# Layer norms by a power on GpSimd instead of Sqrt on ScalarE, and half of a projection's products on ScalarE, in a graph network of four residual layers

## The chip, the cores and the metric

The kernel runs on one core of one Trainium2 chip. The metric is the device time of one execution in microseconds, given as the median of several runs. Four compute engines share the core's on-chip memory (SBUF): TensorE (PE in the profile, with its weight loads as PEld), VectorE (DVE), ScalarE (ACT) and GpSimd (POOL). A fifth sequencer, SyncE (SP), only issues DMAs here. Each engine works through its own queue of instructions in order, and waits there on semaphores of the others. PSUM is the memory into which TensorE writes.

## What is computed

A graph of N = 3327 nodes with 512 features each passes through four layers. Every layer adds the result of a graph operation to its input and normalises each row over its 512 features. Cut to what matters:

```python
def _layernorm(x, axis=-1, eps=1e-5):
    m = jnp.mean(x, axis=axis, keepdims=True)
    v = jnp.var(x, axis=axis, keepdims=True)
    return (x - m) / jnp.sqrt(v + eps)

x = _layernorm(x + gat(x, adj, heads=8))               # layer 0
x = _layernorm(x + sage(x, adj, 64))                   # layer 1
x = _layernorm(x + elu(gat(x, adj, heads=8)))          # layer 2
x = _layernorm(x + elu(gat(x, adj, heads=4)))          # layer 3
```

(The two names stand for the longer functions of the reference.) In `gat`, each head projects x by its own weights to h, forms a score `leaky_relu(si + sj)` for every pair of nodes, masks it by the adjacency, takes the softmax over a row, and multiplies it by h. In `sage`, the mean over the first 64 neighbours of a row is projected, goes through a leaky ReLU and is added to a projection of the row itself. A norm is needed for each of 3327 rows in each of four layers, and with it one factor 1/sqrt(v + eps) a row.

## The kernel before

Rows are padded to 3328, which is NT = 26 tiles of 128 rows; a half is HALF = 13 tiles. The work runs in stages that follow each other; the times are from the start of the profiled span, read off the trace:

- projection of layer 0, to about 124 us;
- attention of layer 0, to about 953;
- layer 1, first part (norm of layer 0, two projections, L1173 to L1245), to about 1161;
- layer 1, second part: for each of 26 slabs of 128 rows, TensorE accumulates mask times features (L1295), `output` (L1270) finishes the slab and calls `norm_rows`, and the projection of layer 2 runs in between as jobs; to about 1600. A mask product kt (L1167, VectorE) is what TensorE takes as weights there;
- attention of layer 2, to about 2395;
- `third` (L1331): finish and norm of layer 2, projection of layer 3; to about 2541. This is called the third projection below, and it has the two kinds of steps that the change touches;
- attention of layer 3, its first half of rows to 2865, its second to 3211. While the second half runs, the first half's rows are finished and normalised as jobs (`later`, L1402), and after it the last rows (L1484 to L1531).

*The norm.* `norm_rows` (L146 to L161) takes one or two tiles. For each: VectorE's bn_stats (L152) and bn_aggr (L153) leave mean and variance in `mv`. Then, once for all of them: ScalarE takes Sqrt of the variance plus eps into `rs` (L154), VectorE takes the reciprocal (L155), and a scalar_tensor_tensor (L158) makes minus mean times factor. Last, ScalarE applies scale and bias to each tile in place (L161). It is called 59 times: 13 times with two tiles in layer 1's first part, 26 times with one tile in its second part, 13 times with two in the third projection, 7 times in the last attention. For the last half of the rows, L1488 and L1526 do the same as L154 with `mv4` and `rs4` (three times), and `factors` (L1468 to L1472) the same as L155 and L158.

*The finish of a layer.* `finish_steps` (L165) loads a tile of attention sums h (from `hd`, on SP) and of the layer's input xr (L177, issued by POOL), multiplies h by the reciprocal row sums (L182, VectorE), takes Exp on ScalarE (L189) for the elu, makes the residual sum in two steps on VectorE (L197, L198) and calls `norm_rows`.

*The third projection* goes over the 26 tiles in pairs. A pair's rows are stored to `x3` (SP). `project1` turns a tile round on TensorE (four transposes to `pt`, L267), ScalarE copies it to SBUF (L268), VectorE sums it for a mean (L269). `project2` multiplies it by the weights into two PSUM banks `pw`, sixteen matmuls (L277): each bank holds two heads of 128 columns and some score columns. ScalarE takes Exp of score columns into `dc` (L278) and copies others (L281). VectorE multiplies each bank by `dc`, a factor for each row and head, into `vt` in SBUF (L283), one instruction for each bank; SP stores `vt` as the value rows (L289). The layers of four and of eight heads share these functions; layer 0 and layer 2 have eight heads of 64 columns.

The pools allow two tiles of each `pw` bank and of `pt`, three of `vt` and `xT`, ten of h, six of xr. ScalarE keeps one set of function tables at a time: where the next function isn't in it, the compiler puts an ACT_TABLE_LOAD ahead.

*The order of the work.* TensorE's order is written by hand: it is in manual schedule, and runs in the order in which the program emits it. On the other engines a scheduler places the instructions by what is ready, apart from those in `tc.keep_in_program_order`, so an edit can move instructions that it doesn't name. The order on an engine is fixed once the kernel is built.

*POOL's order* in layer 1's second part holds loads of carries (`cy`, L1123) and of `xi` (L1272); at the start of the third projection, two memsets (`piece_columns`, L254 and L256); in all stages, xr loads.

Of the kernel before, what the change touches and what calls it, by code (L numbers as in the profile page):

```python
# [7 lines left out]
F32 = mybir.dt.float32  # L8
# [4 lines left out]
AF = mybir.ActivationFunctionType  # L13
ALU = mybir.AluOpType
# [4 lines left out]
P = 128  # L19
LN_EPS = 1e-5  # L20
# [6 lines left out]
def _row_pieces(n):  # L27

    return [(0, n)] if n % 16 == 0 else [(0, n // 16 * 16), (n // 16 * 16, n)]
# [3 lines left out]
def kernel(  # L33
# [10 lines left out]
    nc = tc.nc  # L44
# [21 lines left out]
    const = ctx.enter_context(tc.tile_pool(name="const", bufs=1))  # L66
# [15 lines left out]
    for g in range(4):  # L82
# [6 lines left out]
    nc.gpsimd.memset(onecol[:, 31:32], 1.0)  # L89
    below0 = const.tile([P, 1], F32, name="below0")  # L90
    nc.gpsimd.memset(below0, -200.0)
    eps = const.tile([P, 1], F32, name="eps")
    nc.gpsimd.memset(eps, LN_EPS)
    valid = const.tile([P, 1], F32, name="valid")
    nc.gpsimd.memset(valid, 1.0)
    nc.gpsimd.affine_select(out=valid, in_=valid, compare_op=ALU.is_gt, fill=0.0, base=LAST,
                            pattern=[[0, 1]], channel_multiplier=-1)

    c1 = const.tile([P, 2, 16], F32, name="c1")
    c1a = const.tile([P, 2, 4], F32, name="c1a")  # L100
    iv = ident.rearrange("p (x c) -> p x c", c=8)
# [17 lines left out]
    def load_tile(dst, src, t, eng):  # L119

        if src.shape[0] == N and t == NT - 1 and LAST < P:
            nc.gpsimd.memset(dst, 0.0)
            for a, z in _row_pieces(LAST):
                eng.dma_start(out=dst[a:z, :], in_=src[t * P + a:t * P + z, :])
        else:
            eng.dma_start(out=dst, in_=src[t * P:(t + 1) * P, :])
# [16 lines left out]
            eng.dma_start(out=t[:, :, e, :FW], in_=src[:, e * FW:(e + 1) * FW].rearrange("(c p) m -> p c m", p=P))  # L143


    def norm_rows(pool, ys, t0):  # L146
        n = len(ys)
        st = pool.tile([P, 4, 6], F32, name="st")
        mv = pool.tile([P, 4, 2], F32, name="mv")
        rs = pool.tile([P, 4, 2], F32, name="rs")  # L150
        for s, y in enumerate(ys):
            nc.vector.bn_stats(out=st[:, s, :], in_=y)  # L152
            nc.vector.bn_aggr(out=mv[:, s, :], in_=st[:, s, :])  # L153
        nc.scalar.activation(rs[:, :n, 0], mv[:, :n, 1], AF.Sqrt, bias=eps)  # L154
        nc.vector.reciprocal(rs[:, :n, 0], rs[:, :n, 0])  # L155
        if t0 + n == NT:
            nc.vector.tensor_tensor(rs[:, n - 1, 0:1], rs[:, n - 1, 0:1], valid, op=ALU.mult)
        nc.vector.scalar_tensor_tensor(rs[:, :n, 1], mv[:, :n, 0], -1.0, rs[:, :n, 0],  # L158
                                       op0=ALU.mult, op1=ALU.mult)
        for s, y in enumerate(ys):  # L160
            nc.scalar.activation(y, y, AF.Identity, bias=rs[:, s, 1:2], scale=rs[:, s, 0:1])  # L161
# [3 lines left out]
    def finish_steps(pool, xin, layer, t0, n, hbufs=6, eng=nc.sync, xbufs=None, xpool=None, ebufs=None, pinned=False,  # L165
                     together=False):
        H, D = layer.H, layer.D
        ys, xs, steps = [], [], []

        def load():  # L170
            for t in range(t0, t0 + n):
                xr = xpool.tile([P, F], F32, name="xr", tag="hb") if xpool else \
                    pool.tile([P, F], F32, name="xr", bufs=xbufs)
                h = pool.tile([P, F], F32, name="h", bufs=hbufs)
                load_tile(h, hd, t, eng)
                ys.append(h)
                load_tile(xr, xin, t, nc.gpsimd)  # L177
                xs.append(xr)

        def divide(s):  # L180
            h = ys[s]
            ins = nc.vector.tensor_tensor(h.rearrange("p (h d) -> p h d", h=H), h.rearrange("p (h d) -> p h d", h=H),  # L182
                                          rec[:, t0 + s, :H].rearrange("p (h e) -> p h e", e=1).to_broadcast([P, H, D]),
                                          op=ALU.mult)
            if pinned and t0 > 2:
                tc.keep_in_program_order(ins)
            if layer.elu:
                e = pool.tile([P, F], F32, name="e", bufs=ebufs)
                ins = nc.scalar.activation(e, h, AF.Exp)  # L189
                if pinned and layer.li == 2 and (t0, s) == (2, 0):  # L190
                    tc.keep_in_program_order(ins)
                xs.append(e)

        def add(s):
            h, xr = ys[s], xs[s]
            if layer.elu:
                nc.vector.scalar_tensor_tensor(xr, xs[n + s], 1.0, xr, op0=ALU.min, op1=ALU.add)  # L197
                nc.vector.scalar_tensor_tensor(h, h, 0.0, xr, op0=ALU.max, op1=ALU.add)  # L198
            else:
                nc.vector.tensor_tensor(h, h, xr, op=ALU.add)  # L200

        steps.append(load)
        if pinned or together:
            steps += [lambda s=s: divide(s) for s in range(n)] + [lambda s=s: add(s) for s in range(n)]
        else:
            for s in range(n):
                steps += [lambda s=s: divide(s), lambda s=s: add(s)]
        steps.append(lambda: norm_rows(pool, ys, t0))
        return ys, steps

# [21 lines left out]
    class Layer:  # L232
# [39 lines left out]
        def project2(self, pool, bank, wsb, xT, t):  # L272
            H, D = self.H, self.D
            pw = [bank(e) for e in range(2)]
            for c in range(FC):
                for e in range(2):
                    nc.tensor.matmul(pw[e][:, :FW + H], xT[:, c, :], wsb[:, c, e, :], start=c == 0, stop=c == FC - 1)  # L277
            nc.scalar.activation(self.dc[:, t, :], pw[1][:, FW:FW + H], AF.Exp, scale=ALPHA)  # L278
            vt = pool.tile([P, H, D], F32, name="vt")
            for e in range(2):  # L280
                nc.scalar.copy((self.rc, self.qc)[e][:, t, :], pw[e][:, FW:FW + H])  # L281
                hs = slice(e * H // 2, (e + 1) * H // 2)
                nc.vector.tensor_tensor(vt[:, hs, :], pw[e][:, :FW].rearrange("p (h d) -> p h d", d=D),  # L283
                                        self.dc[:, t, hs].rearrange("p (h e) -> p h e", e=1)
                                        .to_broadcast([P, H // 2, D]), op=ALU.mult)
            vv = vt.rearrange("p h d -> p (h d)")
            n = P if t < NT - 1 else LAST
            for a, z in _row_pieces(n):
                (nc.gpsimd if self.li == 0 else nc.sync).dma_start(out=self.vd[t * P + a:t * P + z, :], in_=vv[a:z, :])  # L289
# [1041 lines left out]
    def third(first):  # L1331
        with tc.tile_pool(name="col3", bufs=1) as cp:
# [5 lines left out]
            with tc.tile_pool(name="p_w", bufs=1, reuse_waits="tile") as wp, \  # L1338
# [23 lines left out]
                for t0 in range(0, NT, 2):  # L1362
# [4 lines left out]
                    for s, y in enumerate(ys):  # L1367
                        t = t0 + s
# [22 lines left out]
            with tc.tile_pool(name="f3", bufs=2) as fp, tc.tile_pool(name="f4", bufs=1) as gp:  # L1391
                g = gp.tile([P, HALF, F], F32, name="g")
                st = gp.tile([P, HALF, 2, 6], F32, name="st4")
                mv = gp.tile([P, HALF, 2], F32, name="mv4")
                rs = gp.tile([P, HALF, 2], F32, name="rs4")
# [71 lines left out]
                def scale(q0, n, keep, every):  # L1467
                    def factors():  # L1468
                        qs = slice(q0, q0 + n)
                        keep(nc.vector.reciprocal(rs[:, qs, 0], rs[:, qs, 0]))  # L1470
                        keep(nc.vector.scalar_tensor_tensor(rs[:, qs, 1], mv[:, qs, 0], -1.0, rs[:, qs, 0],
                                                            op0=ALU.mult, op1=ALU.mult))  # L1472

                    def one(q):
                        y = g[:, q, :]
                        if q % every == 1:
                            keep(nc.scalar.activation(y, y, AF.Identity, bias=rs[:, q, 1:2], scale=rs[:, q, 0:1]))
                        else:
                            keep(nc.vector.tensor_scalar(y, y, rs[:, q, 0:1], rs[:, q, 1:2], op0=ALU.mult, op1=ALU.add))
                        store(y, HALF + q, q)  # L1480

                    return [factors] + [lambda q=q: one(q) for q in range(q0, q0 + n)]

                def slots(q0, n, pt, e):  # L1484
                    keep = tc.keep_in_program_order if e == 1 else lambda ins: ins
                    qs = slice(q0, q0 + n)
                    if e == 2:
                        return [lambda: nc.scalar.activation(rs[:, qs, 0], mv[:, qs, 1], AF.Sqrt, bias=eps)] + \  # L1488
                            scale(q0, n, keep, 3)
                    y = g[:, qs, (NS - 1) * P:]  # L1490
                    h = fp.tile([P, 4, P], F32, name="h", bufs=2)
# [28 lines left out]
                keep = tc.keep_in_program_order  # L1520
                for _, _, parts in lasts:
                    parts[1]()
                for k, (q0, n, parts) in enumerate(lasts):
                    for f in parts[2:]:
                        f()
                    keep(nc.scalar.activation(rs[:, q0:q0 + n, 0], mv[:, q0:q0 + n, 1], AF.Sqrt, bias=eps))  # L1526
                    if k > 0:
                        for f in scale(*lasts[k - 1][:2], keep, 2):
                            f()
# [191 lines left out]
```

## Time and profile before

| | us |
|---|---|
| median of 3 runs (lowest, highest) | 3238.24 (3236.37, 3240.77) |
| the profiled execution | 3230.94 |
| its span in the trace | 3229.1 |
| PE busy | 3137.4 (97%) |
| DVE busy | 2626.5 (81%) |
| ACT busy | 2295.1 (71%) |
| POOL busy | 266.6 (8%) |
| ACT table loads, 145 at 1.283 | 186 |
| of them in the third projection, 32 | 41 |
| Sqrt of `norm_rows` (L154), 59 at 0.295 | 17.4 |
| reciprocals of `norm_rows` (L155), 59 at 0.160 | 9.5 |
| products to `vt` (L283), all three projections, 156 at 0.417 | 58.7 |

The busy time of an engine is the sum of its instructions; register, branch, semaphore and DMA-issuing work isn't in it. A group of instructions in the profile is given as line, engine, operation, the tiles it writes and reads with their sizes, the count, then busy time and mean ns of one, and after a bar the idle time of the engine just before them with what ended most of it. A line of a window gives the busy time of PE, PEld, DVE, ACT and POOL in a stretch of the span (instructions in brackets), then the granted share of TensorE's full clock, the DMA engines' busy share, and GB/s. A line of the waits gives who waited for whom: us in total, times, longest. A line of the chain gives the start, the duration, and the engine and line of a piece of the work that ended last.

### The profile page before, as it was taken

The numbers are of one execution on the slowest core, as the hardware profiler recorded it, in microseconds if no ns is written. First come the engines' busy times: TensorE is split into PE (matmuls) and PEld (weight loads), VectorE is DVE, ScalarE is ACT, GpSimd is POOL, SyncE is SP. The second block draws the span as 40 slices with busy tenths as digits, with TensorE's granted clock in tenths as the row PEclk, the third lists the DMA queues.
The fourth block names the chain that finished last, engine by engine and source line by source line (L and its number), as shares of the span: only waits on it lengthen the run. The fifth ranks groups of instructions, "written<-read, shape, count | busy, mean of one in ns | idle before, by whom it ended". The sixth has DMA issues, their size and how long they took to land. (4 is left out here: it accounts for less than half of the span.)

```text
span 3229.1 us, 44980 instructions
## 1 busy us (share of the span) xinstructions
PE 3137.4 (97%) x17910; PEld 1602.3 (50%) x17910; DVE 2626.5 (81%) x2316; ACT 2295.1 (71%) x1855; POOL 266.6 (8%) x414
## 2 busy tenths in 40 slices
PE   8899999999999999999999999999989999999997
PEld 7643343333334467777744333333347655555444
DVE  5799999999987655555499999999999666677887
ACT  1388888899883234444398988899988655568896
POOL 3110000000000111111220000000011000010110
PEclk9999999999999999999999999999999999999998
DMA  9742113111024345555441111011137211122212
GB/s 360 272 149 80 41 51 137 59 45 42 25 87 138 104 127 133 134 142 152 120 135 42 41 35 39 20 42 42 32 107 242 85 43 43 43 59 89 85 47 69
DMA packets 358321, 301.80 MB, mean 93 GB/s; under 512 B 232756, under 2 KB 291966, under 8 KB 356575
## 3 DMA queue, kind: packets, MB, share of 16 engines
q1 hardware_dynamic: 325727, 187.73, 19.9%
q0 software_dynamic: 26864, 103.50, 10.0%
q10 hardware_dynamic: 5520, 7.69, 0.7%
q8 instruction: 142, 2.33, 0.3%
q14 instruction: 68, 0.56, 0.1%
HBM read 221.97 MB, written 76.84 MB: 93 GB/s over the span
## 5 line engine op out<-in xcount | busy, mean ns | idle before, releaser
L834 ACT ACTIVATE y<-t,bi,sc 128x3328 fp8e4<-128x3328 f32 (+1 forms) x520 | 1336.9, 2604 | 100.0 <-PE pd L811 47.8
L855 PE MATMUL po<-t,vj 128*64 128x448 f32 (+1 forms) x6656 | 1272.9, 522 | 14.6 <-DVE t L833 14.5
L855 PEld LDWEIGHTS po<-t,vj 128*64 128x64 f32 x6656 | 461.0, 137 | 687.8 <-issue 617.6
L470 PE MATMUL po<-t,vj 128*128 128x448 f32 (+1 forms) x1456 | 523.3, 516 | 6.2 <-DVE ob L500 3.6
L408 DVE SCALAR_TENSOR_TENSOR t<-rba,qc,mk 128x1664 f32<-128x1664 f32 (+2 forms) x234 | 408.2, 1753 | 127.7 <-PE po L470 88.2
L413 ACT ACTIVATE y<-t,bi,sc 128x1664 fp8e4<-128x1664 f32 (+2 forms) x234 | 374.3, 1617 | 182.5 <-DVE t L408 170.8
L470 PEld LDWEIGHTS po<-t,vj 128*128 128x128 f32 x1456 | 272.1, 190 | 241.5 <-issue 149.8
L833 DVE SCALAR_TENSOR_TENSOR t<-rba,qc,mask 128x3328 f32<-128x3328 f32 (+1 forms) x130 | 381.1, 2987 | 5.7 <-PE po L855 4.9
L833 DVE SCALAR_TENSOR_TENSOR t<-rbb,qc,mask 128x3328 f32<-128x3328 f32 (+1 forms) x130 | 379.9, 2982 | 6.8 <-PE po L855 3.2
L833 DVE SCALAR_TENSOR_TENSOR t<-rbb,qc,mk 128x3328 f32<-128x3328 f32 (+1 forms) x130 | 379.2, 2981 | 6.7 <-PE po L855 4.5
L833 DVE SCALAR_TENSOR_TENSOR t<-rba,qc,mk 128x3328 f32<-128x3328 f32 (+1 forms) x130 | 379.7, 2986 | 5.7 <-PE po L855 3.4
L1295 PE MATMUL acc<-zs,kt 128*128 128x512 f32 x1352 | 360.2, 420 | 0.0
L277 PE MATMUL pw<-wsb,xT 128*128 128x264 f32 (+1 forms) x1248 | 301.7, 397 | 8.8 <-DVE vt L283 7.3
L1295 PEld LDWEIGHTS acc<-zs,kt 128*128 128x128 f32 x1352 | 256.0, 190 | 51.8 <-PE pk L1146 0.8
L811 PE MATMUL pd<-y,sden 128*32 128x384 fp8e4 (+1 forms) x3328 | 270.2, 343 | 0.0
L277 PEld LDWEIGHTS pw<-wsb,xT 128*128 128x128 f32 x1248 | 242.1, 197 | 50.9 <-issue 6.5
L1153 ACT CAST pk<-cy 128x512 f32<-128x512 bf16 x169 | 99.1, 587 | 222.6 <-DVE kt L1167 216.1
L1167 DVE SCALAR_TENSOR_TENSOR kt<-pk,mb 128x512 fp32r<-128x512 f32 x169 | 115.5, 684 | 115.4 <-PE pk L1164 114.2
L811 PEld LDWEIGHTS <-sden 128*32 128x32 bf16 x3328 | 89.1, 95 | 165.3 <-issue 149.9
L283 DVE TENSOR_TENSOR vt<-pw,dc 128x256 f32<-128x256 f32 x156 | 58.7, 417 | 70.5 <-ACT dc L278 64.7
L1193 PE MATMUL pz<-wn,xT 128*128 128x512 f32 x208 | 96.0, 605 | 5.9 <-DMA wn<-in_wnT_dram 5.5
L1123 POOL DMA_DIRECT2D cy<-ctd x91 | 68.0, 747 | 371.1 <-ACT pk L1153 304.7
(249 smaller groups left out, 2234.2 us busy)
## 6 DMA issues: line engine op xcount, KB each, us to landing
raw<-in_adjT_dram SPq DMA_DIRECT2D x67, 416.0 KB
vj<-v SPq DMA_DIRECT2D x169, 128.0 KB
cy<-ctd POOLq DMA_DIRECT2D x78, 256.0 KB, 4.3
h<-hd SPq DMA_DIRECT2D x61, 256.0 KB
v<-vt SPq DMA_DIRECT2D x50, 256.0 KB
xr<-x POOLq DMA_DIRECT2D x45, 256.0 KB, 3.2
md<-mask SPq DMA_DIRECT2D x26, 416.0 KB
mb<-md SPq DMA_DIRECT2D x169, 64.0 KB
```

What stands on the lines that cost most here:

```text
L277: nc.tensor.matmul(pw[e][:, :FW + H], xT[:, c, :], wsb[:, c, e, :], start=c == 0, stop=c == FC - 1)
L408: ins = nc.vector.scalar_tensor_tensor(t[:, :w], rb[:, lo:lo + w], self.qc[:, j, h:h + 1], mask_at[0](j, i0 + lo, w), op0=ALU.max, op1=ALU ...
L413: nc.scalar.activation(y[:, :w], t[:, :w], AF.Sigmoid, bias=self.bi[:, j, h:h + 1], scale=self.sc[:, j, h:h + 1], saturate=False)
L470: nc.tensor.matmul(po[c][k * D:(k + 1) * D, :z - a_], vj[:, j % 2, k * D:(k + 1) * D], ts[k][:, a_:z], start=j == 0, stop=j == NT - 1)
L811: nc.tensor.matmul(pd[c][32 * kk:32 * kk + 32, :w_], lhsT, rhs, start=(kk, c) not in seen, stop=last and j == NT - 1)
L833: nc.vector.scalar_tensor_tensor(to, ro, self.qc[:, j, h:h + 1], m, op0=ALU.max, op1=ALU.mult)
L834: nc.scalar.activation(yo, to, AF.Sigmoid, bias=self.bi[:, j, h:h + 1], scale=self.sc[:, j, h:h + 1], saturate=False)
L855: nc.tensor.matmul(po[c][k * D:(k + 1) * D, :z - a_], vj[:, j % 2, x_:x_ + D], t[:, k, a_:z], start=j == 0, stop=j == NT - 1)
L1153: nc.scalar.copy(pks[k % 2], carry[b, t // 4 * 4][:, t % 4:t % 4 + 2, :])
L1167: nc.vector.scalar_tensor_tensor(kt, pk, NEIGHBOURS, mb[:, t:t + 2, :], op0=ALU.is_le, op1=ALU.mult)
L1193: nc.tensor.matmul(pz, xT[:, c, :], wn[:, c, :], start=c == 0, stop=c == FC - 1)
L1295: nc.tensor.matmul(acc, kts[b, t][:, s * P:(s + 1) * P], zs(t, c), start=t == 0 and c == 0, stop=t == NT - 1 and c == 1)
```

## The change

Three edits go together.

1. The factor 1/sqrt(v + eps). A new function `rsqrt` has POOL add eps to the variance and raise the sum to the power of -0.5 (tensor_scalar, then tensor_tensor with a constant tile that is filled with -0.5). `norm_rows`, L1488 and L1526 call it in place of ScalarE's Sqrt; VectorE's reciprocals (L155 and L1470) are dropped, and the constant tile `eps`. The two calls for the last half were or could be held in program order; the new ones are not.
2. In `project2` of layer 3 only, bank 1 (heads 2 and 3) is taken out of PSUM by ScalarE, with one multiplication by a column of `dc` for each head, in place of one VectorE instruction for the bank. Bank 0 stays on VectorE.
3. The xr loads of layer 2's finish (26 tiles) are issued by SP in place of POOL.

```diff
+    power = const.tile([P, 8], F32, name="power")
+    nc.gpsimd.memset(power, -0.5)
...
+    def rsqrt(out, var):
+        n = out.shape[-1]
+        return [nc.gpsimd.tensor_scalar(out, var, LN_EPS, None, op0=ALU.add),
+                nc.gpsimd.tensor_tensor(out, out, power[:, :n], op=ALU.pow)]
+
     def norm_rows(pool, ys, t0):
...
-        nc.scalar.activation(rs[:, :n, 0], mv[:, :n, 1], AF.Sqrt, bias=eps)
-        nc.vector.reciprocal(rs[:, :n, 0], rs[:, :n, 0])
+        rsqrt(rs[:, :n, 0], mv[:, :n, 1])
...
-                load_tile(xr, xin, t, nc.gpsimd)
+                load_tile(xr, xin, t, nc.sync if layer.li == 2 else nc.gpsimd)
...
                 hs = slice(e * H // 2, (e + 1) * H // 2)
+                if self.li == 3 and e:
+                    for h in range(hs.start, hs.stop):
+                        nc.scalar.mul(vt[:, h, :], pw[e][:, (h - hs.start) * D:(h - hs.start + 1) * D], self.dc[:, t, h:h + 1])
+                    continue
                 nc.vector.tensor_tensor(vt[:, hs, :], pw[e][:, :FW].rearrange("p (h d) -> p h d", d=D),
...
-                        keep(nc.vector.reciprocal(rs[:, qs, 0], rs[:, qs, 0]))
...
-                        return [lambda: nc.scalar.activation(rs[:, qs, 0], mv[:, qs, 1], AF.Sqrt, bias=eps)] + \
+                        return [lambda: rsqrt(rs[:, qs, 0], mv[:, qs, 1])] + \
...
-                    keep(nc.scalar.activation(rs[:, q0:q0 + n, 0], mv[:, q0:q0 + n, 1], AF.Sqrt, bias=eps))
+                    rsqrt(rs[:, q0:q0 + n, 0], mv[:, q0:q0 + n, 1])
```

All lines are those of the kernel before.

More of the change, by code (lines that the diff above doesn't have):

```diff
@@ L91 @@
     nc.gpsimd.memset(below0, -200.0)
-    eps = const.tile([P, 1], F32, name="eps")
-    nc.gpsimd.memset(eps, LN_EPS)
     valid = const.tile([P, 1], F32, name="valid")
```

## The prediction

> **What bounds the kernel now.** I read the page's totals first, then the sliced utilisation, then the windows, the waits and the chain of the stage that the change touches most.
>
> ```profile
> PE 3137.4 (97%) x17910; PEld 1602.3 (50%) x17910; DVE 2626.5 (81%) x2316; ACT 2295.1 (71%) x1855; POOL 266.6 (8%) x414
> ```
>
> TensorE (PE) is busy for 97% of the span: 91.7 of 3229.1 us are idle, and no edit here removes a matmul. Only idle PE can be won. Time off ACT or DVE is worth nothing where PE is full, as in the layer-1 stage, where 26 of the 59 norms are (first line: PE 320 of 320 us). It can count in the third projection, 2395 to 2542 us (the others; columns are PE, PEld, DVE, ACT, POOL, clock, DMA share, GB/s):
>
> ```profile
> 1180.00:1500.00 320.00, 320.00 (x1394) 240.38 (x1393) 173.94 (x338) 141.68 (x252) 59.68 (x86) 1.00 0.55 140
> 2395.00:2431.00 36.00, 23.29 (x114) 16.85 (x111) 29.93 (x64) 25.50 (x47) 10.81 (x18) 0.81 0.80 252
> 2431.00:2458.00 27.00, 27.00 (x139) 23.47 (x138) 25.20 (x65) 22.01 (x50) 3.22 (x6) 1.00 0.88 291
> 2458.00:2485.00 27.00, 20.45 (x98) 15.79 (x97) 24.44 (x65) 22.23 (x47) 3.78 (x7) 0.89 0.64 206
> 2395.00:2542.00 147.00, 126.31 (x615) 102.42 (x612) 118.36 (x279) 114.14 (x231) 21.06 (x39) 0.93 0.62 204
> ```
>
> PE is idle for 12.7 us at the start and 6.6 us in the middle, and the clock falls after each (0.81, 0.89). DVE and ACT are near full there. What PE waits for, and who holds DVE:
>
> ```profile
> PE pt L267 <- ACT h L161: 11.8, 4, 8.3
> DVE vt L283 <- ACT dc L278: 11.7, 5, 3.7
> ```
>
> The chain of waits shows ACT's table loads between the norms (2463 to 2468):
>
> ```profile
> 2458.92 0.69 DVE xsum L269
> 2461.57 1.52 ACT h L161 x2
> 2463.11 1.28 ACT L278
> 2465.14 1.28 ACT L154
> 2466.74 1.28 ACT L278
> 2468.11 0.81 ACT h L161
> ```
>
> The groups of table loads and of the norm's Sqrt, over the kernel:
>
> ```profile
> L154 ACT ACT_TABLE_LOAD x45 | 57.7, 1283 | 41.3 <-DVE mv L153 40.8
> L278 ACT ACT_TABLE_LOAD x33 | 42.3, 1283 | 0.6
> L154 ACT ACTIVATE rs<-mv,eps 128x2 f32<-128x2 f32 (+1 forms) x59 | 17.4, 295 | 17.3 <-DVE mv L153 16.6
> ```
>
> **What the Trainium skill says.** "ScalarE: Activation LUTs", section What ACT_TABLE_LOAD costs, gives about 1283 ns per load plus a drain of about 1380. The trace agrees on the load; it shows no such drain (the Sqrt that follows the load of 2402.06 starts at 2403.35), so I count 1.28 us per switch. The same section prices an ACTIVATE at 186 ns + 0.833 ns a column, 93 more per pointer operand, with 93 overlapped back to back. L301 (256 columns from PSUM, constant scale) shows 386 ns against 399 by that rule, so it fits. "GPSIMD Engine Reference", section 3.1, gives 2.6 cycles an element for two-input operations and two software dispatch hops; 8 elements would be nothing, so dispatch sets the price. No page prices power there. Section 8 says that GpSimd shares its SBUF interfaces with VectorE; the trace agrees in kind: L384, one form of TENSOR_SCALAR on POOL, takes 682 to 2683 ns.
>
> **The change, part by part.**
>
> *Removed.* Every Sqrt goes (59 in the groups, 3 in the last half), so that ACT no longer alternates Sqrt with Exp. The built instruction order has 59 table loads against 145: 86 x 1.28 = 110 us of ACT, 32 of the old ones (41 us) in the third projection; 13 Sqrts (3.8) go there too. DVE loses 62 reciprocals of 0.16 us (13, so 2.0 us, in the third projection) and, at layer 3, one of two L283 per tile: 26 x 0.416 = 10.8 us.
>
> *Added on ACT.* 52 products of 128x128 with a pointer scale. By the skill's rule an estimate of 186 + 107 + 93 = 386 ns, 293 if overlapped; I take 0.33: 17 us. ACT in the third projection: 114 - 36 (about 28 loads) - 4 + 17 = 91 of 147 us.
>
> *Added on POOL.* 62 pairs, add eps then power. The trace shows no such operation. Per norm let P be the time from the variance to the factor, both hand-offs in. Below: memset 0.095 and affine_select 0.185 on 128x1, twice, with hand-offs, give 0.6. Above: two L384 at their longest, 5.4 us. I take 1.2 (two at about 0.4 and three hand-offs), and keep 0.6 and 5 for the range. It replaces 1.28 + 0.30 + 0.16 = 1.74 where a load was due, 0.46 where not.
>
> *DVE's new wait.* The next instruction but one on DVE (L158) waits for POOL in order; one of about 0.6 us lies between. Behind it queue the next residual additions and, in layer 1, the mask products kt for which PE waits.
>
> *Third projection, the sum.* PE at full rate takes 3.51 (pw) + 0.44 (pt) = 3.95 us a tile, 102.7 for 26. DVE now takes, at starts 0.60 apart (two L198 in 1.20): 5 x 0.60 + 2 x 0.38 + 0.15 + 0.16 = 4.07, so it is the slower engine. Without the second L283 and the halved reciprocal it is 3.6, with P - 0.6 = 0.6 us of stall per pair 3.9: just at PE's 3.95. Thus:
> - Start: the first norm's variance is there at 2402.8, but its reciprocal waits in DVE's order to 2405.55 and L158 to 2408.97, behind an L182 that waits 2.65 us for its load. In the new order L158 directly follows, so PE starts near 2405, not 2410. The second norm's POOL pair is queued behind the memsets of sden and sm (2.0 + 0.8 us from 2416.2), ready near 2417, not 2423. PE runs without gaps from about 2424 instead of 2430: -6.
> - Middle: PE's 6.6 us of idle came from three loads in a row (3.8 us) and DVE's lag. I count 5 of it: -5.
> - End: the last dc (L278) sat behind two loads (2531.67, 2534.76): -2 to -3.
> - Clock and rounding: -1.
>
> Together -14 (-6 if the stalls only shift, -19 if PE is full to the end). The xr loads move from POOL to SP (26 x 0.54 us of issue): SP has the stores and loads of the stage in its order, two xr loads sit between value loads at the end of layer 2's attention. Those value loads wait for PE to free their buffers until 2352 anyway, and SP's own work in the stage is issue only; I take 0, at worst +2. The value store now waits for ACT too: it is needed only after the stage.
>
> *Layer 3's attention.* PE is full to 2865 and waits 10.4 us after; seven norms of the first half lose up to two loads each there, ACT being 65 to 78 of 83 us busy. PE's gaps at 2949, 3033, 3040 and 3147 us are only partly behind these. I take -2 (+3 to -5).
>
> *Layer 1.* 13 norms at its start, 26 inside: PE is full after 1000 us. POOL's power stands before the weight load wn at 954, for which PE waits 5.5 us: +0.7. DVE already waits 18.2 us (21 times) for the Sqrt there with PE full: 0. If that cover were gone, it would cost 26 x (P - 0.46) = 19 us at 1.2. On POOL the pair stands behind the xi load and the cy loads; the xi load of the slab near 1311 us was issued at 1311.00, its variance came at 1312.41, so nothing holds the pair.
>
> *Tail.* Last factors: load and Sqrt out, two POOL operations in: 0 (0.5 either way).
>
> **Sum.** -14 - 2 + 0.7 = -15.3. The profiled run took 3230.94 us (span 3229.1 and 1.84 around it), so 3215.6; it stands 7.3 us below the median of the runs, 3238.24. From the median: **3223 us**.
>
> **The rivals.**
>
> *R1, slower: power on POOL is long.* From P = 4.5 us the third projection gains nothing: a pair takes DVE 7.2 + 3.9 = 11.1 us, 144 for 13, against 146 used now. At P = 5 it is 151: +5. In layer 1 the kt wait of DVE after the factor is about 2.5 us and one kt (0.68), so each slab loses 5 - 3.2 = 1.8 us, 47 for 26; PE's buffers hold perhaps half: +24. Sum +29: 3267 us. For it: L384's 2.7 us, power's price unknown. Against: two elements a partition only, and POOL is 8% busy.
>
> *R2, same: the stage is bound by its transfers or by the order.* DMA share is 0.88 at 291 GB/s in the one gapless stretch, and four L182 wait 5.3 us for h. Then only the start (-3) and the tail (-2) remain: 3233 at P near 1, 3238 if DVE's stall eats them; I put it at 3235. For it: SP now issues xr too. Against: PE ran at full rate at that share.
>
> *R3, more: all gaps close.* The third projection at 102.7 us from 2405, -19, layer 3 -5: about 3213 us. Against: several h loads are late whatever ACT does.
>
> *R4, no effect off the path:* ACT is 71% busy and PE 97%, so 110 us of ACT are hidden. True for layers 1 and 0, but the waits above end in ACT, so I fold its chance into R2.
>
> **How the numbers follow.** Forecast 3216 to 3231 (P from 0.6 to 1.8, third projection -9 to -19): 0.55. R3, 3206 to 3216: 0.12. R2 with R4, 3231 to 3241: 0.19. R1, above 3241: 0.14. About 0.2% (6.5 us) can be told from no change, so faster means under 3231.8. Faster: 0.55 + 0.12 + 0.02 of R2's edge = 0.69; same 0.17; slower 0.14. The range leaves out a third of R3 below and most of R1 above: 3210 to 3243.
>
> **What would show it.** Right: table loads in the third projection from 32 to under 8; the window from 2395 us shorter by 10 us or more, with PE idle for under 10 us in it instead of 20.7; L283 waiting for dc under 4 us; PE's first pt L267 wait near 3 instead of 8.3. P right: the POOL power under 0.6 us and DVE's factor wait for POOL under 0.7 each. R1 right: POOL's power over 2 us, kt late, PE under 100% in layer 1. R2 right: waits for loads take the place of those for ACT. Wrong altogether: the third projection is shorter by 14 us and the total isn't.

## The result, and the profile after

The changed kernel takes 3221.37 us (median of 4 runs, 3220.14 to 3223.41) against 3237.76 us (4 runs) for the kernel before: a ratio of 0.9949, 95% interval 0.9933 to 0.9964, so 16 us less (12 to 22). The forecast was 3223. The profiled execution took 3223.41 us (span 3221.7). The profile of before came from a short execution, 3230.94 us, so the two spans differ by only 7.4 us; each kernel was therefore profiled a second time (3232.16 us before, 3221.47 us after), and stages are compared over both pairs.

All lines of the kernel after are shifted: L283 of before is L291, L277 is L281, L158 is L162, L161 is L165; the two POOL steps are L148 and L149, ScalarE's products L289. The totals of the page after:

```profile
PE 3135.2 (97%) x17910; PEld 1596.6 (50%) x17910; DVE 2609.5 (81%) x2228; ACT 2185.6 (68%) x1759; POOL 322.5 (10%) x512
```

ACT is 109.5 us less busy than before (2295.1), DVE 17 less, POOL 56 more, and PE is busy for 2 us less. Of 109.5 us only 16 reach the end.

Windows of the kernel after: the stretch of layer 1 that was shown of before, and the third projection from the last L819 of layer 2's attention to the first value product of layer 3's (129.40 us):

```profile
1180.00:1500.00 320.00, 320.00 (x1394) 240.04 (x1393) 172.15 (x322) 96.78 (x201) 76.64 (x125) 1.00 0.56 141
2407.00:2536.40 129.40, 117.09 (x571) 97.78 (x564) 102.67 (x231) 79.98 (x231) 25.89 (x40) 0.95 0.68 228
```

The same stretch of the kernel before:

```profile
2397.90:2535.70 137.80, 118.25 (x570) 98.53 (x563) 111.86 (x262) 104.99 (x215) 20.61 (x38) 0.93 0.64 209
```

So PE's idle time there went from 19.6 to 12.3 us, and the stretch lost 8.4 us. ACT fell by 25 us and DVE by 9. In layer 1's window ACT fell by 45 us with PE full in both.

Waits of PE and of DVE in the kernel after, between 2380 and 2545 us:

```profile
PE pt L271 <- ACT h L165: 7.4, 4, 4.8
DVE rs L162 <- POOL rs L149: 7.6, 9, 1.2
DVE vt L291 <- ACT dc L282: 7.1, 5, 2.1
```

Three groups of the kernel after, on POOL and ACT:

```profile
L149 POOL TENSOR_TENSOR rs<-rs,power 128x2 f32<-128x2 f32 (+3 forms) x62 | 42.8, 691 | 4.9
L148 POOL TENSOR_SCALAR rs<-mv 128x2 f32<-128x2 f32 (+3 forms) x62 | 21.2, 342 | 242.5 <-DVE mv L158 162.4 <-DVE mv L1516 74.1 <-ACT pc L378 5.8
L289 ACT ACTIVATE vt<-pw,dc 128x128 f32<-128x128 f32 x52 | 16.4, 368 | 0.1
```

The table loads of the third projection, which were 32, are 4:

```profile
L421 ACT ACT_TABLE_LOAD x2 | 2.6, 1283 | 0.0
L193 ACT ACT_TABLE_LOAD x1 | 1.3, 1283 | 0.0
L282 ACT ACT_TABLE_LOAD x1 | 1.3, 1283 | 0.0
```

One norm of the third projection as the timeline after has it (start, duration; in brackets the idle time before and its releaser):

```profile
2439.89 0.17 DVE L158 BATCH_NORM_AGGREGATE mv<-st 128x2 f32<-128x6 f32 x1
2439.98 0.65 DVE L201 SCALAR_TENSOR_TENSOR xr<-e,xr 128x512 f32<-128x512 f32 x1
2440.22 0.49 POOL L148 TENSOR_SCALAR rs<-mv 128x2 f32<-128x2 f32 x1 [7.76 <-DVE mv L158]
2440.80 0.71 POOL L149 TENSOR_TENSOR rs<-rs,power 128x2 f32<-128x2 f32 x1
2441.54 0.16 DVE L162 SCALAR_TENSOR_TENSOR rs<-mv,rs 128x2 f32<-128x2 f32 x1 [0.91 <-POOL rs L149]
```

From the variance (2440.06) to the factor's use (2441.54) it is 1.48 us: P of the prediction, and the median of the stage's 13 pairs. DVE has one instruction to put in between, as foreseen, and stalls for 0.91 us. In layer 1's slabs P is shorter (variance at 1299.76, L162 at 1300.83, 1.07 us). There each norm has one tile, so the power works on one column and takes 0.57 us instead of 0.71, and the addition takes 0.22 us instead of 0.49 beside DVE's additions of two SBUF operands. The second difference agrees in kind with the Trainium skill ("GPSIMD Engine Reference", section 8, Key points), which says that GpSimd shares its SBUF interfaces with VectorE and contends with VectorE instructions that have two SBUF inputs.

### The profile page after: what moved, and what is told of

It reads as the page before. It is cut to its first block, busy times and chain, and to the rows that moved or that the text cites. A ratio compares the mean times of both kernels' runs of the same rounds, so it can differ in the third digit from the quotient of the medians.

```text
span 3221.7 us, 44965 instructions
## 1 busy us (share of the span) xinstructions
PE 3135.2 (97%) x17910; PEld 1596.6 (50%) x17910; DVE 2609.5 (81%) x2228; ACT 2185.6 (68%) x1759; POOL 322.5 (10%) x512
## 3 DMA queue, kind: packets, MB, share of 16 engines
q1 hardware_dynamic: 329471, 194.55, 20.7%
## 5 line engine op out<-in xcount | busy, mean ns | idle before, releaser
L281 PE MATMUL pw<-wsb,xT 128*128 128x264 f32 (+1 forms) x1248 | 297.7, 393 | 11.8 <-DVE vt L291 8.1
L819 PE MATMUL pd<-y,sden 128*32 128x384 fp8e4 (+1 forms) x3328 | 270.2, 343 | 0.0
L281 PEld LDWEIGHTS pw<-wsb,xT 128*128 128x128 f32 x1248 | 238.4, 194 | 54.8 <-issue 6.5
L819 PEld LDWEIGHTS <-sden 128*32 128x32 bf16 x3328 | 89.0, 95 | 166.7 <-issue 151.2
L291 DVE TENSOR_TENSOR vt<-pw,dc 128x256 f32<-128x256 f32 x130 | 49.8, 417 | 78.1 <-ACT dc L282 76.0
```

The source lines that it names most:

```text
L819: nc.tensor.matmul(pd[c][32 * kk:32 * kk + 32, :w_], lhsT, rhs, start=(kk, c) not in seen, stop=last and j == NT - 1)
```

## The experiments

Each kernel was timed in 5 rounds against the kernel before on the same chip, apart from the changed kernel (4 runs) and the two repeats. The first table gives ratio, interval and the ratio as us of 3238. The second gives five stages in us, each of one profiled execution, read off from the start of TensorE's first or last instruction of a line: layer 1's first part (first pz to first acc), its slabs (first to last acc), the third projection as above, layer 3's attention (first to last L470), and what follows the last matmul of the last unit's values. The profiled execution can lie at the edge of its kernel's runs: that of Sqrt in the first part was the fastest of six, that of the second power the fastest of 14, that of Sqrt in the slabs the slowest of six.

| kernel | ratio to before | us |
|---|---|---|
| changed kernel | 0.9949 (0.9933 to 0.9964) | -16 |
| power alone | 0.9974 (0.9965 to 0.9983) | -8 |
| products alone | 1.0007 (0.9999 to 1.0016) | +2 |
| xr on SP alone | 1.0002 (0.9994 to 1.0010) | +1 |
| power and products | 0.9965 (0.9953 to 0.9978) | -11 |
| power and xr on SP | 0.9967 (0.9954 to 0.9979) | -11 |
| changed, Sqrt in layer 1's first part | 0.9930 (0.9917 to 0.9943) | -23 |
| the same, addition on VectorE | 0.9944 (0.9930 to 0.9959) | -18 |
| changed, Sqrt in layer 1's slabs | 0.9956 (0.9943 to 0.9970) | -14 |
| changed, Sqrt in layer 3 | 0.9971 (0.9962 to 0.9981) | -9 |
| changed, second power | 1.0000 (0.9992 to 1.0008) | 0 |

| kernel | first part | slabs | third projection | attention 3 | end |
|---|---|---|---|---|---|
| before, two profiles | 196.7, 197.1 | 440.7, 446.6 | 137.8, 137.8 | 579.5, 582.2 | 18.5, 18.7 |
| changed, two profiles | 200.9, 200.3 | 441.4, 442.3 | 129.4, 128.4 | 572.2, 572.3 | 20.7, 20.5 |
| power alone | 200.1 | 440.3 | 136.0 | 573.1 | 18.3 |
| products alone | 197.1 | 447.2 | 141.6 | 580.3 | 18.6 |
| xr on SP alone | 197.1 | 447.0 | 135.7 | 582.2 | 20.8 |
| power and products | 200.2 | 440.4 | 133.3 | 572.3 | 18.6 |
| power and xr on SP | 199.6 | 441.1 | 132.3 | 573.2 | 20.5 |
| changed, Sqrt in first part | 197.3 | 440.2 | 128.6 | 572.3 | 20.3 |
| the same, addition on VectorE | 196.8 | 441.1 | 130.0 | 572.3 | 20.6 |
| changed, Sqrt in slabs | 199.9 | 446.7 | 128.3 | 572.3 | 20.3 |
| changed, Sqrt in layer 3 | 199.9 | 444.3 | 129.2 | 581.6 | 20.3 |
| changed, second power | 203.1 | 442.0 | 135.3 | 572.9 | 21.7 |

**The parts apart.** The power alone: the products' branch and the move of xr are left out.

```diff
-                load_tile(xr, xin, t, nc.sync if layer.li == 2 else nc.gpsimd)
+                load_tile(xr, xin, t, nc.gpsimd)
...
-                if self.li == 3 and e:
+                if False:
```

> Only the norms' factor is changed (power on POOL); products of heads 2 and 3 stay on VectorE, xr loads on POOL. My theory (table loads and VectorE's work hold the third projection together): VectorE needs 4.3 us a tile with the stall for POOL, over TensorE's 3.95, so about half of the change's 16 us: 8 us faster than before. Rival A (the table loads are all of it): 16 us faster. Rival B (the products are most of it): under 4 us faster.

Measured: 8 us faster (6 to 11), as the theory said, but not where it said. The third projection is only 1.8 us shorter; most of the gain lies in layer 3's attention (573.1 against 579.5 and 582.2). Rivals A and B fall.

The products alone, in the kernel before:

```diff
+                if self.li == 3 and e:
+                    for h in range(hs.start, hs.stop):
+                        nc.scalar.mul(vt[:, h, :], pw[e][:, (h - hs.start) * D:(h - hs.start + 1) * D], self.dc[:, t, h:h + 1])
+                    continue
```

> Only the products of heads 2 and 3 in the last projection go to ScalarE; Sqrt and its table loads stay, xr loads on POOL. My theory: ScalarE, with 41 us of table loads in the third projection, goes from 114 to 131 us busy of 147 and becomes what TensorE waits for as often as VectorE did: between 2 us faster and 5 slower than before, likeliest 0. Rival A (the table loads are all of it): 3 us slower or more. Rival B: 10 us faster or more.

Measured: 2 us slower (0 to 5), within the theory's bounds. Rival B is out; rival A, 3 us slower or more, is not excluded by this run and falls only with the power alone. The third projection takes 141.6 us instead of 137.8. With the table loads in place ACT has no room for 16 us more; its window, from the end of layer 2's attention, has ACT busier than DVE:

```profile
2407.60:2549.20 141.60, 119.83 (x571) 100.08 (x564) 106.45 (x244) 116.46 (x270) 21.04 (x38) 0.93 0.62 205
```

The xr loads alone, in the kernel before:

```diff
-                load_tile(xr, xin, t, nc.gpsimd)
+                load_tile(xr, xin, t, nc.sync if layer.li == 2 else nc.gpsimd)
```

> Only the xr loads of layer 2's finish go from POOL to SP. My theory: no change, within 3 us. Rival (SP's order delays h loads at the start of the third projection, or the xr loads were late behind POOL's memsets): 3 to 6 us slower or faster.

Measured: no change (2 us less to 3 more): 2.1 us less in the third projection, 2 more at the end.

The changed kernel with xr back on POOL:

```diff
-                load_tile(xr, xin, t, nc.sync if layer.li == 2 else nc.gpsimd)
+                load_tile(xr, xin, t, nc.gpsimd)
```

> The changed kernel, but xr loads stay on POOL: there the power pairs stand behind xr loads that wait for VectorE. My theory: as the changed kernel, 16 us faster than before, or 1 to 3 us less where a pair stands behind a waiting xr load. Rival (the move is what makes the power usable): 8 us less.

Measured: 11 us faster than before, so some 5 less than the changed kernel, between the two. The third projection is 4.4 us longer (133.3 against 128.9, the mean of the two). Its first two power pairs are split by xr loads and, at the second, stand behind the memsets. The first pair on POOL in that kernel:

```profile
2410.74 0.23 POOL L148 TENSOR_SCALAR rs<-mv 128x2 f32<-128x2 f32 x1 [1.30 <-DVE mv L158]
2411.16 0.57 POOL L126 DMA_DIRECT2D xr<-x  x1 [0.18 <-issue]
2411.75 0.80 POOL L149 TENSOR_TENSOR rs<-rs,power 128x2 f32<-128x2 f32 x1
```

The fourth combination, power and xr move with the products on VectorE:

```diff
-                if self.li == 3 and e:
+                if False:
```

> The changed kernel with all products of the last projection on VectorE again: power on POOL and xr loads on SP. So far, against before: power alone 8 us faster, power and products 11, all three 16, xr alone 0. My theory: with xr on POOL the power pairs stand behind xr loads that wait for VectorE, so the move counts as soon as the power is on POOL: 12 to 13 us faster than before. Rival (the move counts only where VectorE is relieved too): 8 us faster, as the power alone.

Measured: 11 us faster (7 to 15), which lies between theory and rival and decides nothing by itself. The stages speak for the theory: the third projection goes from 136.0 (power alone) to 132.3 without any products moved, against 2.1 us less for the move without the power. The end takes 2 us of it back.

**The places apart.** In the changed kernel, Sqrt and reciprocal are put back for the norms of one place. The body is the same for the first two; what selects the calls differs (layer 0's finish for the first, `output` for the second).

```diff
-        rsqrt(rs[:, :n, 0], mv[:, :n, 1])
+        if root:
+            nc.scalar.activation(rs[:, :n, 0], mv[:, :n, 1], AF.Sqrt, bias=eps)
+            nc.vector.reciprocal(rs[:, :n, 0], rs[:, :n, 0])
+        else:
+            rsqrt(rs[:, :n, 0], mv[:, :n, 1])
...
-        steps.append(lambda: norm_rows(pool, ys, t0))
+        steps.append(lambda: norm_rows(pool, ys, t0, layer.li == 0))
```

> The changed kernel, with Sqrt on ScalarE and the reciprocal on VectorE for the 13 norms of layer 1's first part alone, where no Exp runs between them. My reading of the traces so far: that part takes 200 to 201 us with the power and 197 with Sqrt, so this is 3 to 4 us faster than the changed kernel, 20 us faster than before. Rival (the 4 us are spread between executions): as the changed kernel, 16 us faster than before.

Measured: 23 us faster than before (18 to 27). The first part is back at 197.3 us, so the power costs 3 to 4 us there. Between its time and the changed kernel's the intervals overlap; the shorter stage is shown, the whole 7 us are not.

```diff
-                    norm_rows(sp, [y], t)
+                    norm_rows(sp, [y], t, True)
```

> The changed kernel, with Sqrt and reciprocal for the 26 norms of layer 1's slabs alone. My reading now: the longer way by Sqrt delays a turned load (yx) on which VectorE waits in order, and TensorE then misses a mask product for 4 us and loses clock: 6 us slower than the changed kernel, 10 faster than before. Rival (what I predicted: TensorE is full there, 0): as the changed kernel, 16 us faster than before.

Measured: 14 us faster than before (10 to 18), in which both the expected 10 and the rival's 16 lie. In its profile the slabs take 446.7 us, with the wait that was expected. The same wait is in the second profile of the kernel before, for PE and for DVE (1165 to 1605 us):

```profile
PE pk L1164 <- DVE kt L1167: 4.0, 1, 4.0
```

```profile
DVE xT L263 <- DMA yx<-x: 3.9, 1, 3.9
```

DVE waits in order for a turned load of one slab, and the mask products behind it are late once. This is in four of the five profiles with Sqrt in the slabs (3.9 to 4.8 us) and missing in the first one of before (0.2). In the two profiles of the changed kernel DVE's wait is 1.4 and 2.3, and in no profile with the power there is it longer than 2.4. Its cost in the median wasn't resolved.

For layer 3, `root` is true where `layer.li == 3`, and L1488, L1526 and `factors` are as before:

```diff
-                        return [lambda: rsqrt(rs[:, qs, 0], mv[:, qs, 1])] + \
+                        return [lambda: nc.scalar.activation(rs[:, qs, 0], mv[:, qs, 1], AF.Sqrt, bias=eps)] + \
```

> The changed kernel, with Sqrt and reciprocals for the norms within and after layer 3's attention alone. My reading now: the attention of layer 3 takes 572 to 573 us up to its last unit in three kernels with the power and 580 to 582 in three without: 7 us slower than the changed kernel, 9 faster than before. Rival (what I predicted, 2 us): 14 us faster than before.

Measured: 9 us faster than before (6 to 12), as expected of my second reading; my predicted 2 us fall. The attention takes 581.6 us instead of 572.3.

**The length of P.** One more power of 1.0 behind each:

```diff
-                nc.gpsimd.tensor_tensor(out, out, power[:, :n], op=ALU.pow)]
+                nc.gpsimd.tensor_tensor(out, out, power[:, :n], op=ALU.pow),
+                nc.gpsimd.tensor_tensor(out, out, unit[:, :n], op=ALU.pow)]
```

> The changed kernel with one more power on POOL (by 1.0, so the value stays) behind each, some 0.75 us longer from variance to factor in all 62 norms. My theory (VectorE stalls in order, cover differs by stage): third projection +8 us, first part of layer 1 +3, its slabs and layer 3 about +1: 12 us slower than the changed kernel, 4 faster than before. Rival A (the wait is covered everywhere): 2 us slower, 14 faster than before. Rival B (POOL's time counts in full): 46 us slower, so 30 slower than before.

Measured: no change against before, 16 us lost against the changed kernel (11 to 22 from the two intervals). That is more than the 12 expected, though 12 lies in the range; both rivals are out. The third projection lost 6.4 us, the first part 2.5. DVE's waits for POOL in that kernel (2400 to 2545 us) are 1.4 us each instead of 0.84, and in sum 6.4 us longer, as much as the stage:

```profile
DVE rs L165 <- POOL rs L152: 14.0, 10, 1.7
```

The way round, P shortened: from the version with Sqrt in the first part, eps is added on VectorE.

```diff
-        return [nc.gpsimd.tensor_scalar(out, var, LN_EPS, None, op0=ALU.add),
+        return [nc.vector.tensor_scalar(out, var, LN_EPS, None, op0=ALU.add),
```

> The version with Sqrt in layer 1's first part, and everywhere else the addition of eps on VectorE (one instruction of some 0.16 us) so that POOL has only the power: from variance to factor 0.95 instead of 1.15 us. My theory: VectorE is at TensorE's pace in the third projection and gains 0.2 us of stall but pays 0.16 us: no change against that version, so 24 us faster than before. Rival (the POOL hop is what counts, as the 16 us for a second power of 0.7 us suggest): 4 us more, 28 faster than before.

Measured: 18 us faster than before (13 to 23), not told from the version it starts from. The rival's 28 is out, and the 24 of the theory lies just outside too. DVE's waits for POOL in the third projection fall from 7.7 us in 9 to 5.1 in 10, and its own 0.16 us a norm takes about as much (130.0 against 128.6 us).

**Repeats.** The kernel before and the changed one, without an edit.

> The kernel before, unchanged, for a second profile. The first one was of an execution 7 us below its median. If that is the missed mask product in layer 1's slabs, this one has about 447 us there instead of 440.7 where it lies near the median; if not, 441 and the time elsewhere.

Measured: 3232.16 us, close to the median of the 12 runs beside it (3233.41), with 446.6 us in the slabs: as expected of an execution near the median. But its time up to layer 1 was 4.6 us shorter than in the first profile and its layer 3 attention 2.7 longer, so the missed mask product alone doesn't make the distance between that profile and the median.

> The changed kernel, unchanged, for a second profile: the stages as in the first, third projection 129 us, attention of layer 3 up to its last unit 572, layer 1's first part 200 to 201, slabs 440 to 442.

Measured: 3221.47 us, every stage within 1 us of what was expected of it.

## Why the prediction was right, point by point

The total was right (3223, measured 3221), the terms only in part, and that they add up so well is luck: the third projection gave 5 us less than foreseen and layer 3's attention nearly 7 more. Mean of both profiles of each kernel:

| step | predicted us | measured us |
|---|---|---|
| third projection | -14 | -8.9 |
| layer 3's attention | -2 | -8.6 |
| layer 1, first part | +0.7 | +3.7 |
| layer 1, slabs | 0 | -1.8 |
| tail | 0 | +2.0 |
| sum | -15.3 | -13.6 |

The slabs' -1.8 lies within the spread of the two profiles before (440.7 and 446.6). And the table doesn't account for the whole 16 us. The rest of the span is 4.6 us longer in the pair after, so that the profiled spans differ by 9.0 us in the mean and the medians by 16; where the other 7 lie isn't known.

*Bound.* Right: with 110 us off ACT the busy time of PE fell by 2 us only, and its idle time by 5 us in one pair of profiles and 8.5 in the other. R4's thought holds for most of the 110.

*Removed and added.* 145 table loads became 59, and the third projection kept 4 of 32. The products took 368 ns each, two in 0.62 us; 0.33 was taken.

*Signs.* Of those named, the table loads came true (4, under 8). Others fell short: the window lost 8.9 us, not 10 or more, PE's idle time in it is 12.3 us, not under 10, its first wait for the norm 4.8, not near 3, and L291 waits 7.1 us for dc, not under 4.

*P.* The value taken, 1.2 us, is met in layer 1's slabs (1.07) and short for the third projection (1.48), where POOL's addition runs beside DVE and the power has two columns. "Dispatch sets the price" therefore doesn't hold for the power: 0.57 us for one column and 0.71 for two, and the single calls with four and seven columns take 1.18 and 1.52. The sign that the text named, a power under 0.6 us, came true for one column only, the mean is 0.69; and DVE's waits for POOL, to be under 0.7 each, are 0.84 on average in the third projection.

*Third projection, mis-sized.* "PE runs without gaps from about 2424 instead of 2430: -6" came out as -4.8 (the second pair of tiles starts 19.9 us after layer 2's attention instead of 24.7). "In the new order L158 directly follows" did not come true: two multiplications L186 that wait for their h, 1.29 and 0.68 us, still stand ahead of the first factor (2412.52 and 2413.99 us).

"I count 5 of it" for the middle and 1 for the clock came out as -3.8: PE's longest wait there, for an Exp of ScalarE (L318, L326 after), fell from 4.3 to 2.0 us, and PE still waits for ScalarE's normalised rows. "The last dc sat behind two loads: -2 to -3" is -0.3: that dc was late for VectorE, but PE had value products to do and didn't wait for it.

The step that failed is the claim that DVE at 3.9 us a tile is "just at PE's 3.95". Its stall for POOL was sized about right: 7.6 us in nine waits and 1.2 in a tenth, so 0.68 a pair against 0.6. But the sum has no term for what else DVE does in the stage, and none for its waits for ScalarE. Of the 129.4 us after, DVE is busy for 102.7, which alone is 3.95 a tile, and waits 8.8 for POOL and 13.6 for ScalarE (dc, xT, rc and the Exp). An engine at the pace of another leaves no slack for such hold-ups; the kernel with the second power shows that they count, as 6.4 us more of DVE's stall made the stage 6.4 us longer. Between 2428 and 2450 us the chain after runs through DVE, POOL and ACT, and PE is not in it; some of its pieces:

```profile
2439.38 0.59 DVE xsum L273
...
2440.22 0.51 POOL rs L148
...
2440.80 0.72 POOL rs L149
...
2442.45 0.80 ACT h L165
```

*Three edits, one effect.* I added up power and products and took 0 for xr. The third projection shows that they depend on each other: power alone -1.8, products alone +3.8, xr alone -2.1, all three -8.9. The products need ACT free of table loads: without the power they cost 3.8 us, with it they gain 2.7 (136.0 to 133.3). The move of the xr loads depends less on the other two: in this stage it is worth 2.1 us alone, 3.7 with the power and 4.4 with both. These are single profiles; two of the same kernel differ by up to 1.0 us in this stage.

*Layer 3's attention, mis-sized.* I took "-2 (+3 to -5)" since the gaps are "only partly behind these". Most were: PE's idle time in this attention is 7.3 and 6.9 us in the two profiles before and 0.9 in both after. The kernel before, around the first gap (timeline, other lines left out):

```profile
2933.88 1.28 ACT L154 ACT_TABLE_LOAD   x1
...
2935.49 1.28 ACT L413 ACT_TABLE_LOAD   x1
...
2938.47 1.51 ACT L161 ACTIVATE h<-h,rs 128x512 f32<-128x512 f32 x2
...
2939.88 0.93 SPq L133 DMA_DIRECT2D out_dram<-h  x2
...
2945.46 0.95 SPq L126 DMA_DIRECT2D h<-hd  x2
...
2948.08 0.69 DVE L182 TENSOR_TENSOR h<-h,rec 128x512 f32<-128x512 f32 x1 [6.65 <-DMA h<-hd]
2948.80 0.62 DVE L500 COPY ob<-po 128x448 f32<-128x448 f32 x1
...
2949.48 1.96 PE L470 MATMUL po<-t,vj 128*128 128x448 f32 x4 [1.77 <-DVE ob L500]
```

ACT normalises a pair late, its store and so the next load into that buffer are late, DVE waits for the load in order for 6.65 us, and the copy that frees PE's bank stands behind it. In the kernel after the load is issued at 2933 to 2934 us, DVE waits 0.40 us for it, and no such gap is left:

```profile
2936.05 0.69 DVE L186 TENSOR_TENSOR h<-h,rec 128x512 f32<-128x512 f32 x1 [0.40 <-DMA h<-hd]
```

DVE's waits for h in this attention are 12.8 and 10.4 us in the two profiles before, 3.3 and 2.5 after, and 11.0 with Sqrt put back in layer 3 alone. That it is the table switches that make it late, and not the hand-off between the engines, is argued from the order of these lines; that the Sqrt does, is shown.

*Layer 1.* The first part was mis-sized: +3.7 instead of +0.7. There Sqrt needs no table switch beyond the first, so P of over 1 us replaces 0.46. That the power costs it is shown by the two kernels with Sqrt there (197.3 and 196.8 us). Most of it is seen: near 1123 and 1140 us PE waits for VectorE's zs and ScalarE's h and xT, 2.1 to 3.0 us in sum in the seven profiles with the power there and 3.9 with the second power; the six with Sqrt there have no such wait. The longest wait of DVE for POOL, 3.0 us at 952, where a cy load that waits for PE stands between addition and power, comes before this stage's first pz and isn't in the 3.7. "DVE already waits for the Sqrt there with PE full: 0" held for the slabs in the window shown.

*R1* has the right mechanism and the wrong point. I put it at P = 4.5, from 144 us for 13 pairs against the 146 of the whole window. But the window holds start and end too. At 0.7 us more per norm, 6.4 of 8.9 us are gone: by a straight line through these two, an estimate, the third projection gains nothing from a P of about 2.5 us on.

*Open.* The stretch from the last slab to the end of layer 2's attention, in which no norm is left to do but the last slabs', takes 796.5 to 803.5 us in the fourteen profiles and is 3.6 us longer in the pair after than in the pair before; no edit sorts it. And the end is 2 us longer in every kernel with xr on SP. The records show where: the last DMA is issued equally early, 12.6 to 12.7 us after the start of the last value matmul in twelve profiles of both kinds, but GpSimd's closing DRAIN instruction takes 5.0 to 5.2 us in the five profiles with xr on POOL and 6.7 to 7.3 in the nine with xr on SP. Why it does isn't known.

## What to carry to other kernels

Find which idle time of the bound engine ends in the work that an edit removes, stage by stage, and follow one level further: a late normalisation can be a late store, a late load, and a stall of an engine that frees something else. A switch of function tables that disappears pays twice, by itself and by making room on the engine for other work. Moving a small step to a slow but idle engine is right where it replaces a switch and wrong where it doesn't: mixing both ways by place gave the best median here, 3214 us, though its interval overlaps that of the changed kernel.

## What the runs showed of the hardware

A power by tensor_tensor on GpSimd takes 0.56 to 0.59 us on 128x1 (27 times), 0.71 us or more on 128x2 (33 times, median 0.72), and 1.18 and 1.52 us in the single calls on 128x4 and 128x7.

The addition before it takes 0.21 to 0.24 us in 43 of the 60 norms of one or two columns, and 0.49 us or more in the other 17 (once 1.77). In each of these 17, and in none of the 43, a VectorE instruction with two SBUF inputs runs beside it for 0.4 us or longer. VectorE's kt products, which take one input from PSUM, run beside 14 of the short ones.

The drain that the prediction looked for beside the table loads doesn't show: of the 144 loads that follow other work of ScalarE in the profile before, 114 have at most 0.05 us of idle time both ahead of them and behind them. A switch costs ScalarE's queue 1.28 us there.
